# A Mamba and MoE layer on one core: the gate weights' split and one delta times u given to GpSimd, with a new written order

## The chip, the cores and the metric

The kernel runs on one core of a Trainium2 chip. The metric is the device time of one execution in microseconds (us); the median of three runs is taken. A profile is one such execution, recorded by the hardware.

The engines have short names in the profile: PE is TensorE (matmuls; PEld its weight loads), DVE is VectorE, ACT is ScalarE, POOL is GpSimd, SP is SyncE, which issues all the DMAs here. Each engine runs its own queue in order and waits for the others by semaphores.

## The reference

The input is 32 sequences of 256 tokens with 128 channels. Everything is float32.

```python
x = L0_attn_x                                  # (32, 256, 128)
x = x + mamba(layernorm(x), ...)
x = x + moe(layernorm(x), ...)

def mamba(x, W_in, conv_w, conv_b, W_x, W_dt, b_dt, A_log, D, W_out):
    xi, res = split(x @ W_in, 2)               # 256 channels each
    u = silu(causal_conv4(xi) + conv_b)
    dbc = u @ W_x                              # delta_r (8), B (16), C (16)
    delta = softplus(dbc[..., :8] @ W_dt + b_dt)
    h_t = exp(delta_t * A) * h_(t-1) + delta_t * B_t * u_t     # 16 states per channel
    y_t = sum over states of h_t * C_t
    return ((y + u * D) * silu(res)) @ W_out

def moe(x, gate_w, w1, w2):                    # 8 experts, the best 2 of each token
    scores = x @ gate_w.T
    cw = softmax over the top 2 scores, 0 for the other experts
    return sum over e of cw[:, e] * (silu(x @ w1[e].T) @ w2[e].T)
```

## The kernel before

**Tiles.** The 32 sequences are worked through in 17 tiles: tiles 0 and 16 hold one sequence, the others two (`EDGE`, `BPT`, line 306). Channels lie on the 128 partitions in two halves, c = 0 and 1. The 16 states of one half are scanned in groups of 1024 columns: two states of two sequences, or in tiles 0 and 16 four states of one sequence. So a tile of two sequences has 16 scans, tiles 0 and 16 have 8, 256 in all.

**Pieces and the order.** The work of a tile is cut into named pieces (`@piece`). `ORDER`, a list written out ahead of time (lines 47 to 284), names tile and piece: `1:sc0` is scan 0 of tile 1. At the end (line 1190) the pieces are issued in that order. An instruction only enters the queue of its own engine, so the list fixes the order on each engine, on SP's queue too; between engines only data dependences and free buffers hold an instruction back. `need` (line 527) puts a table load on ScalarE wherever the list goes over from one activation function's table to another's; so the order also sets how many of these there are (L530).

The pieces that matter here, with their lines and engines:

- `ldx`, `ldr`: loads of x (SP); two buffers. `st1..`, `sa1`: statistics of the first layernorm and their aggregation (VectorE, L538, L544); `rs1`: its scale, with a power (GpSimd, L554 to L557); `ap1`: the normalization itself (ScalarE, L563); `tr1`, `hi1`, `nl1`, `lo1`: the transposition into a high and a low float32r part (TensorE, ScalarE).
- `cv0`, `cv1`: convolution and input projection in one (TensorE, L635); `u0`, `u1`: silu (ScalarE, L649); `wx`: u @ W_x (TensorE, L658); `sb`, `rh`, `nr`, `rl`: that result for B and C, and in two parts for delta (ScalarE, L671, L685, L695); `bcd`: B and C to DRAM (SP); `rb`, `rc`: a row of B or C read back and spread over all partitions (SP, L778).
- `zz`: the product with W_dt (TensorE, L728), which needs `kdt`, the split of W_dt (VectorE, L497); `sp0`, `sp1`: softplus, giving delta (ScalarE, L739); `gp`, `gs`: the gate res and its silu (TensorE, ScalarE, L703, L718).
- `du0`, `du1`: delta times u of one channel half (GpSimd, L793) into the SBUF tile `dus`; `dp0`, `dp1`: its copy into the PSUM tile `du`, of which there is one (ScalarE, L799). Tile 0 uses `dq0` and `dq1` in their place: VectorE writes delta times u straight into PSUM (L807).
- `in0..15`: du times a row of B into PSUM (VectorE, L818); `dk0..15`: the decays exp(delta A) (ScalarE, L760; nine buffers); `sc0..15`: the scan (VectorE, L825) into one of three state buffers h; `cm0..15`: h times a row of C, in place (GpSimd, L836); `ys0..15`: h transposed and added up over states in PSUM (TensorE, L844), which frees the state buffer.
- `yc`, `yz`, `yt`, `ye`, `op`, `x2`: gate, transposition and output projection. Then the second layernorm (`st2..` to `lo2`), the router (`gt` on TensorE; `sc`, `r0` to `r3`, `rw1`, `rw2` on VectorE) and per expert `wi`, `si`, `wo`, `as`, `aa`: first product (TensorE, L1125), silu (ScalarE, L1138), second product (TensorE, L1146), scaling (ScalarE, L1158), sum (GpSimd, L1164). In the last tiles `ad` adds on VectorE (L1169).

**Weights.** They are loaded once, in the list between the first tile's pieces. Weights used in float32r are split into a high part (a cast) and a low part (the rest): `split`, line 356, on VectorE. `kgt` (line 515) splits the gate weights of the router, 128x8; they are needed first by `0:gt`. `kw0`, `kw1` split the halves of w1, `kwr` the gate half of W_in. `kdg` (line 510) makes the diagonal with D that `ys0` of each half multiplies with u.

Of the kernel before, what the change touches and what calls it, by code (L numbers as in the profile page):

```python
# [8 lines left out]
F32 = mybir.dt.float32  # L9
# [62 lines left out]
1:st22 2:sc4 2:rc4 2:cm4 0:aa7 2:rc5 2:rb6 2:rc7 2:rb7 5:ldx 2:rc12 2:rc6 1:st21 2:in5 1:st23 2:dk13 0:wo5
3:wx 3:sb 3:rh 1:x2 2:dk12 0:wo3 2:ys2 2:sc5 1:sa2 1:rs2 2:in6 3:nr 2:ys3 0:wo1 2:dk14 0:as5 3:rl 1:ap2 0:as3
2:ys4 0:wo6 2:sc6 2:cm5 2:in7 1:tr2 1:hi2 5:st10 2:sc7 1:nl2 2:ys5 2:dp1 1:lo2 2:in8 1:gt 1:sc 2:sc8 1:wi30
2:in9 1:r3 0:aa3 0:as1 1:wi10 1:si10 1:si30 2:cm6 2:cm7 0:aa5 2:ys6 2:sc9 5:st12 2:in10 1:r0 1:wi11 1:wi70
1:si11 1:wi40 0:as6 1:wi00 1:si70 1:wi20 1:si40 1:si00 1:si20 2:ys7 2:sc10 1:wi50 1:si50 2:yc0 1:wi31 1:si31
1:wi51 1:si51 2:in11 1:r1 2:rb12 2:rb14 3:zz 4:rs1 4:ap1 3:sp0 3:sp1 2:cm8 2:rc11 2:rb15 2:ys8 1:wo1 1:wi01
2:sc11 2:in12 0:aa1 2:cm9 2:rc14 3:bcd 2:rb13 2:cm10 1:r4 3:du0 2:cm11 2:dk15 3:dk2 1:rx 1:r2 1:rw0 1:rw4
2:yz0 2:ys9 2:sc12 2:cm12 0:aa6 1:wi71 1:wi60 2:ys10 2:ys11 1:si01 1:si71 1:si60 2:in13 1:rw1 2:sc13 2:rc15
2:ldr 3:rb1 2:rc13 3:rb4 3:rc0 2:in14 3:rb0 1:rw2 2:sc14 2:in15 1:rw3 2:cm13 3:rc3 3:rb3 2:cm14 1:wi61 1:si61  # L80
1:wi41 1:si41 1:wi21 1:si21 3:dk1 1:wo0 1:wo6 1:as6 3:dk3 1:as1 1:aa1 1:aa6 2:ys12 2:sc15 2:cm15 3:dp0 3:in1
5:st11 3:dk5 2:ys13 3:sc1 3:in0 2:yt0 1:wo3 1:as3 2:ye0 1:as0 3:dk0 2:px 2:ys14 3:sc0 1:wo4 2:ys15 1:wo5 3:dk6
2:yc1 3:dk4 3:dk8 3:rb2 0:sto 3:in2 5:st13 3:rc2 3:rc1 6:ldx 1:aa3 2:yz1 2:yt1 3:cm0 1:aa0 3:cm1 2:ye1 3:sc2
2:op 3:ys0 2:st20 4:tr1 3:in3 2:st21 2:st22 3:sc3 2:st23 3:in4 2:sa2 1:as4 1:wo2 3:ys1 3:sc4 3:dk7 1:as5 1:aa5
3:cm2 2:rs2 3:dk11 3:dk10 4:hi1 4:nl1 1:wo7 3:ys2 1:as2 4:lo1 2:x2 3:dk12 2:ap2 4:cv0 3:rb5 3:in5 5:sa1 3:sc5
3:rc5 3:rb7 3:rb6 3:rc4 3:rc6 2:tr2 4:u0 3:in6 6:st10 2:hi2 3:cm3 4:gp0 2:nl2 3:ys3 4:cv1 4:gs0 2:lo2 3:dk9
3:sc6 1:aa2 1:as7 3:dk13 3:cm4 5:rs1 3:du1 3:cm5 3:in7 3:dp1 3:dk15 6:st13 3:ys4 3:sc7 3:cm6 3:rc12 3:rc7 2:gt
2:sc 3:in8 2:r0 3:rb13 3:ys5 2:wi00 4:gp1 2:si00 2:wi30 4:u1 4:wx 4:gs1 2:wi60 3:ys6 3:sc8 3:cm7 5:ap1 2:si60
2:si30 4:sb 2:r1 3:in9 2:r3 3:sc9 3:ys7 2:wi20 2:si20 4:rh 2:wi70 2:wi61 4:nr 2:si70 3:yc0 4:rl 2:si61 3:dk14
3:in10 2:r2 3:sc10 2:wi50 3:cm8 3:ys8 3:cm9 3:ys9 4:zz 2:wi21 1:aa4 2:r4 2:rx 2:rw0 3:ldr 3:rc13 3:rb12 4:bcd  # L90
3:rc11 4:rb1 3:in11 4:sp0 2:wi71 4:sp1 2:wi31 2:si21 2:si31 2:si71 2:rw4 2:rw1 3:sc11 3:in12 3:cm10 3:ys10
2:wi01 5:tr1 2:wi40 2:si01 2:si50 2:si40 2:wi10 2:si10 5:hi1 2:wi41 2:wi51 2:rw2 3:sc12 4:du0 1:aa7 3:cm11
3:cm12 2:rw3 3:yz0 3:rb14 3:rc15 3:in13 3:rb15 3:rc14 4:rb4 3:sc13 3:in14 3:cm13 4:rb0 2:wi11 2:si11 2:si51
2:si41 3:ys11 2:wo2 2:wo3 3:ys12 5:nl1 3:yt0 3:sc14 4:rc0 4:rc1 3:cm14 4:dk3 4:dk2 2:as3 2:as2 2:aa3 3:ys13
2:wo1 3:ys14 2:wo0 3:in15 4:dp0 6:st11 4:rb3 3:sc15 4:in0 6:st12 3:cm15 4:rb2 2:aa2 3:ys15 4:dk0 4:sc0 4:cm0
4:in1 5:lo1 3:px 4:dk1 3:ye0 2:wo4 2:as0 2:wo5 3:yc1 3:yz1 2:as1 4:dk5 4:dk7 4:dk9 3:yt1 4:ys0 6:sa1 4:sc1
4:in2 4:sc2 4:in3 3:ye1 3:op 3:st20 4:sc3 3:st23 3:st21 3:st22 4:in4 3:sa2 4:dk4 4:dk6 2:wo7 2:aa1 2:as5
4:dk11 4:cm1 4:ys1 4:sc4 2:aa0 6:rs1 4:du1 4:dk12 2:as7 5:cv0 4:rc4 4:rc3 1:sto 3:x2 4:dk10 7:ldx 4:rc2 4:cm2
4:ys2 4:rb5 4:rb7 4:rc5 4:rb6 4:rc7 5:cv1 5:gp1 4:in5 2:aa7 2:as4 4:dk8 5:u1 5:gp0 5:gs0 3:rs2 3:ap2 5:u0
4:cm3 4:rc11 4:ys3 2:wo6 4:cm4 4:rc6 4:sc5 4:cm5 2:aa5 4:in7 3:tr2 3:hi2 5:wx 5:sb 5:rh 4:ys4 7:st10 4:sc7  # L100
3:nl2 3:lo2 4:in6 4:sc6 4:cm6 4:cm7 4:ys5 5:nr 5:rl 3:gt 3:sc 4:dp1 4:in8 5:gs1 3:wi70 3:si70 2:as6 3:wi50
3:si50 3:r3 4:sc8 3:wi00 3:si00 3:wi30 3:wi40 4:ys6 3:wi60 6:ap1 3:si30 3:r0 3:si40 4:in9 3:si60 2:aa4 4:cm8
3:r4 4:rb13 4:ldr 4:rb12 5:bcd 4:rc12 3:r1 4:sc9 4:in10 5:rb1 3:r2 4:dk13 4:ys7 4:yc0 3:rx 4:dk14 4:sc10
3:wi51 3:wi41 3:wi20 3:si41 3:si51 3:si20 4:in11 4:ys8 7:st13 4:sc11 4:in12 3:wi31 4:cm9 4:rc13 4:rb14 4:ys9
3:wi10 3:si10 3:si31 3:wi01 3:wi11 3:si11 3:wi21 3:si21 3:si01 4:cm10 2:aa6 4:yz0 3:rw0 3:rw4 4:cm11 4:sc12
4:in13 3:rw1 3:wi71 3:si71 3:wi61 3:si61 4:yt0 4:ys10 5:zz 4:sc13 4:in14 3:rw2 3:wo1 4:ye0 6:tr1 5:sp0 3:wo3
4:ys11 5:sp1 3:wo2 4:cm12 4:ys12 5:du0 4:cm13 3:rw3 4:dk15 5:dk0 5:dk1 6:hi1 6:nl1 5:dk3 3:as1 4:sc14 4:rb15
4:in15 7:st11 4:rc14 4:cm14 5:rb4 4:rc15 5:rb0 5:rb3 5:dp0 6:lo1 5:dk7 4:ys13 3:aa1 3:wo5 4:ys14 3:wo0 5:dk4
3:as5 3:as2 4:sc15 4:cm15 3:aa5 4:ys15 3:wo4 4:yc1 3:as0 4:yz1 5:dk2 5:in1 5:rc0 5:rb2 7:st12 5:sc1 5:in0
# [178 lines left out]
def mamba_moe_kernel(  # L288
# [67 lines left out]
    def split(parts, src):  # L356
        nc.vector.tensor_copy(parts[0], src)
        nc.vector.tensor_tensor(parts[1], src, parts[0].bitcast(F32), ALU.subtract)
# [913 lines left out]
```

## Time and profile before

| what | us |
|---|---|
| median of 3 runs | 1044.05 |
| lowest and highest run | 1043.04, 1046.95 |
| the profiled execution, its own time | 1043.46 |
| its span, first to last instruction | 1041.7 |
| first scan starts | 25.92 |
| last scan starts | 1002.96 |

| engine | busy us | share of the span |
|---|---|---|
| VectorE | 967.1 | 93% |
| TensorE | 952.9 | 91% |
| ScalarE | 944.7 | 91% |
| GpSimd | 901.8 | 87% |

Of VectorE's time 584.3 us are the 256 scans (2282 ns each) and 314.9 us their 256 products with B (1230 ns each). Of GpSimd's, 604.2 us are the products with C (2379 ns each).

Rows of the timeline read: start in us, duration in us, engine, source line, operation, output tile <- input tiles, shapes, count; in brackets the idle time of the engine just before, and what it waited for. Where several instructions of one kind follow each other, they are merged into one row. Rows of the waits read: who waited, for whom, us in all, how many times, the longest.

### The profile page before, as it was taken

The numbers are of one execution on the slowest core, as the hardware profiler recorded it, in microseconds if no ns is written. First come the engines' busy times: TensorE is split into PE (matmuls) and PEld (weight loads), VectorE is DVE, ScalarE is ACT, GpSimd is POOL, SyncE is SP. The second block draws the span as 40 slices with busy tenths as digits, with TensorE's granted clock in tenths as the row PEclk, the third lists the DMA queues.
The fourth block names the chain that finished last, engine by engine and source line by source line (L and its number), as shares of the span: only waits on it lengthen the run. The fifth ranks groups of instructions, "written<-read, shape, count | busy, mean of one in ns | idle before, by whom it ended". The sixth has DMA issues, their size and how long they took to land.

```text
span 1041.7 us, 18833 instructions
## 1 busy us (share of the span) xinstructions
PE 952.9 (91%) x6693; PEld 833.6 (80%) x6693; DVE 967.1 (93%) x946; ACT 944.7 (91%) x1893; POOL 901.8 (87%) x676
## 2 busy tenths in 40 slices
PE   6578789899999999999999999999989999899998
PEld 5467678879798888879888887888878788787888
DVE  4999999999999999999999999999999999999963
ACT  6889989989899999989999898989979999899975
POOL 2668888999899999998899999998989999899962
PEclk9789999999999999999999999999999999999999
DMA  7474848668476776847586685858668585865500
GB/s 234 155 258 161 284 167 274 219 215 284 172 256 189 254 257 205 282 157 260 197 266 240 209 268 174 273 175 277 222 196 272 179 279 178 269 232 197 182 11 16
DMA packets 86094, 223.75 MB, mean 215 GB/s; under 512 B 8048, under 2 KB 35312, under 8 KB 85872
## 3 DMA queue, kind: packets, MB, share of 16 engines
q1 hardware_dynamic: 86000, 222.55, 64.5%
q8 instruction: 52, 0.85, 0.3%
q14 instruction: 42, 0.34, 0.1%
HBM read 217.28 MB, written 5.24 MB: 214 GB/s over the span
## 4 chain that ended last, share of the span: by engine, by line
PE 31%; ACT 26%; DVE 21%; POOL 15%; issue 6%; DMA 1%; SPq 0%; DVEq 0%; POOLq 0%; ACTq 0%
DVE h L825 13%; ACT da L760 9%; PE pf L1125 9%; POOL h L836 9%; PE pe L1146 7%; DVE db L818 6%; PE y L844 6%; ACT L530 5%; POOL x L1164 3%; ACT so L1158 3%; PE pc L635 3%; ACT hs L1138 2%; PE po L966 1%; PE pd L658 1%; ACT xn_c L563 1%
## 5 line engine op out<-in xcount | busy, mean ns | idle before, releaser
L836 POOL TENSOR_TENSOR h<-h,rc 128x1024 f32<-128x1024 f32 x255 | 604.2, 2379 | 67.4 <-DVE h L825 56.3
L825 DVE TENSOR_TENSOR_SCAN h<-da,db 128x1024 f32<-128x1024 f32 x256 | 584.3, 2282 | 21.9 <-PE y L844 7.6
L760 ACT ACTIVATE da<-de,a_sb 128x510 f32<-128x510 f32 (+1 forms) x544 | 341.1, 718 | 0.9 <-DVE h L825 0.5
L818 DVE TENSOR_TENSOR db<-du,rb 128x1024 f32<-128x1024 f32 x256 | 314.9, 1230 | 11.2 <-ACT du L799 2.1
L844 PE MATMUL y<-ident,h 128*128 128x128 f32 x2048 | 268.8, 278 | 20.0 <-POOL h L836 19.5
L844 PEld LDWEIGHTS y<-ident,h 128*128 128x128 f32 x2048 | 237.2, 144 | 39.2 <-POOL h L836 26.7
L1146 PE MATMUL pe<-w_sb,hs 128*128 128x128 f32 x2048 | 249.1, 276 | 3.8 <-ACT so L1158 2.8
L1146 PEld LDWEIGHTS pe<-w_sb,hs 128*128 128x128 f32 x2048 | 238.8, 192 | 11.3 <-ACT so L1158 4.4
L1125 PE MATMUL pf<-xt,w_r 128*128 128x512 f32 (+1 forms) x816 | 215.8, 399 | 12.5 <-ACT hs L1138 7.3
L1138 ACT ACTIVATE hs<-pf 128x512 f32<-128x512 f32 (+1 forms) x272 | 144.6, 577 | 40.3 <-PE pf L1125 36.6
L1125 PEld LDWEIGHTS pf<-xt,w_r 128*128 128x128 f32 x816 | 138.6, 189 | 52.9 <-ACT hs L1138 19.7
L1164 POOL TENSOR_TENSOR x<-x,so 128x512 f32<-128x512 f32 (+1 forms) x126 | 157.5, 1250 | 10.5 <-ACT so L1158 9.2
L1158 ACT ACTIVATE so<-pe,cw 128x128 f32<-128x128 f32 x488 | 140.4, 393 | 6.4 <-PE pe L1146 4.1
L530 ACT ACT_TABLE_LOAD x105 | 134.7, 1283 | 1.9
L635 PE MATMUL pc<-xt_r,wc_r 128*128 128x512 f32 (+1 forms) x408 | 99.9, 396 | 1.1 <-ACT xt_r L624 1.1
L635 PEld LDWEIGHTS pc<-xt_r,wc_r 128*128 128x128 f32 x408 | 73.8, 197 | 15.4 <-issue 0.8
L862 PE MATMUL y<-dg_sb,u 128*128 128x128 f32 x256 | 36.4, 285 | 11.7 <-ACT yt L917 6.9
L862 PEld LDWEIGHTS y<-dg_sb,u 128*128 128x128 f32 x256 | 32.6, 195 | 17.0 <-ACT yt L917 10.6
L924 POOL TENSOR_TENSOR g<-yt,g 128x512 f32<-128x512 f32 (+1 forms) x33 | 40.7, 1233 | 5.6 <-ACT yt L917 2.9
L793 POOL TENSOR_TENSOR dus<-de,u 128x512 f32<-128x512 f32 (+1 forms) x32 | 39.8, 1247 | 0.0
L966 PE MATMUL po<-wo_sb,yt 128*128 128x128 f32 x256 | 32.8, 277 | 2.3 <-ACT yt L944 2.2
L966 PEld LDWEIGHTS po<-wo_sb,yt 128*128 128x128 f32 x256 | 30.8, 192 | 4.9 <-ACT yt L944 3.2
(101 smaller groups left out, 716.8 us busy)
## 6 DMA issues: line engine op xcount, KB each, us to landing
rc<-bc SPq DMA_DIRECT2D x205, 512.0 KB, 5.1
rb<-bc SPq DMA_DIRECT2D x187, 512.0 KB, 4.8
xa<-in_x SPq DMA_DIRECT2D x15, 256.0 KB, 4.4
xc<-in_x SPq DMA_DIRECT2D x15, 256.0 KB, 4.4
out<-x SPq DMA_DIRECT2D x15, 256.0 KB, 6.0
w1h<-in_w_t SPq DMA_DIRECT2D x2, 512.0 KB, 7.1
w_sb<-in_w_t SPq DMA_DIRECT2D x1, 1024.0 KB, 7.6
bc<-s SPq DMA_DIRECT2D x32, 32.0 KB, 3.1
```

The source lines that it names most:

```text
L530: nc.scalar.preload_act_table_set(SETS[which])
L635: nc.tensor.matmul(pcv, wc_r[a][:, j, c * P : (c + 1) * P], xt1_r[b][:, : nb[i], o + j : o + j + L], start=(k == 0), stop=(k == 3 * KC - 1),)
L760: nc.scalar.activation(da[:, m, :, 1:], de[:, :, 1:], AF.Exp, scale=a_sb[:, c, n : n + 1])
L818: nc.vector.tensor_mul(db, d["du"].unsqueeze(1).to_broadcast([P, gs[i], tok[i]]), rows["b", i, k])
L825: nc.vector.tensor_tensor_scan(flat(h), da_of(i, k), flat(d["db"]), 0.0, ALU.mult, ALU.add,)
L836: nc.gpsimd.tensor_tensor(h, h, rows["c", i, k], ALU.mult)
L844: nc.tensor.matmul(y[:, q, :], src[:, q * P : (q + 1) * P], ident, is_transpose=True, start=False, stop=last, skip_group_check=True,)
L1125: nc.tensor.matmul(pf, w1_r[a][:, e, f * P : (f + 1) * P], d["xt"][b], start=(k == 0), stop=(k == 2),)
L1138: nc.scalar.activation(d["hs", e][:, f, :], d["pf", e, f], AF.Silu)
L1146: nc.tensor.matmul(pe[:, q, :], hs[:, f, q * P : (q + 1) * P], w2_sb[:, e, f, :], start=(f == 0), stop=(f == FC - 1),)
L1158: nc.scalar.activation(so[:, q, :], d["pe", e][:, q, :], AF.Copy, scale=d["cw"][:, q, e : e + 1])
L1164: nc.gpsimd.tensor_tensor(x2, x2, st[i]["so", e], ALU.add)
```

## The change

`kgt` runs on GpSimd, and so does the product delta times u of channel half 1 in tile 0: `0:dq1` is replaced by `0:du1` and `0:dp1`. `dq0` stays. The tile `dus`, made so far by `du0`, is made by whichever of the two comes first. `ORDER` is replaced as a whole: but for those three pieces it names the same ones, in a different sequence from its first line to its last.

```diff
-    def split(parts, src):
-        nc.vector.tensor_copy(parts[0], src)
-        nc.vector.tensor_tensor(parts[1], src, parts[0].bitcast(F32), ALU.subtract)
+    def split(parts, src, eng=nc.vector):
+        eng.tensor_copy(parts[0], src)
+        eng.tensor_tensor(parts[1], src, parts[0].bitcast(F32), ALU.subtract)
...
     @piece("kgt")
     def _(i):
-        split([gt_r[:, k, :] for k in range(2)], stage["gt"])
+        split([gt_r[:, k, :] for k in range(2)], stage["gt"], nc.gpsimd)
...
     @piece("du1", 1)
     def _(i, c):
         d = st[i]
-        if c == 0:
+        if "dus" not in d:
             d["dus"] = pw.tile([P, DC, tok[i]], F32, tag="du", name=f"dus_{i}", bufs=1)
         nc.gpsimd.tensor_tensor(d["dus"][:, c, :], d["de"][:, c, :], d["u", c], ALU.mult)
```

The first lines of the list before:

```text
0:pm 0:ldx 0:lw0 0:lw1 0:lc0 0:lc1 1:ldx 0:ldp 0:st10 0:st11 0:sa1 0:rs1 0:ap1 0:km1 0:tr1 0:kh1 0:hi1 0:nl1
0:km0 0:kh0 0:lo1 0:kl1 1:st10 1:st11 1:st13 1:st12 0:kl0 0:kwr 0:cv1 0:cv0 1:sa1 1:rs1 3:ldx 3:st10 0:ldd
0:ldk 0:ka 0:u1 1:ap1 1:tr1 0:u0 0:wx 0:gp0 0:sb 0:rh 0:kdt 1:hi1 0:nr 0:rl 0:gs0 1:nl1 0:zz 0:pb0 1:lo1 0:sp0
0:pc0 0:l11 0:ldg 0:ld2 0:l10 2:ldx 2:st10 3:st13 0:kw0 0:kw1 2:st12 0:dq0 2:st11 2:st13 0:in0 2:sa1 0:bcd
0:rc0 0:rc3 0:rb1 0:rc1 0:rb2 0:dk0 0:dk2 0:dk1 0:sc0 0:cm0 0:in1 0:sc1 0:in2 0:kgt 0:sc2 0:dk5 0:dk3 2:rs1
2:ap1 0:kdg 0:cm1 1:gp1 1:cv1 1:cv0 1:u0 0:ys0 1:u1 0:dk4 0:ys1 1:wx 1:rh 1:sb 0:dk6 0:dk7 0:rb3 0:in3 0:dq1
0:sc3 0:in4 0:sc4 0:in6 0:rc7 0:rc2 0:cm2 0:cm3 0:ys2 1:nr 1:rl 0:sc6 1:bcd 0:ldr 0:ys3 1:zz 1:sp0 0:yc0 1:sp1
...
```

and after:

```text
0:pm 0:ldx 0:lw0 0:lc0 0:lc1 0:ldk 1:ldx 0:l11 0:ldo 0:st10 0:st11 0:sa1 0:rs1 0:km0 0:ap1 0:km1 0:tr1 1:st10
0:kh1 0:lw1 1:st12 0:ldp 0:hi1 0:kl1 0:kh0 0:nl1 0:ldd 1:st13 0:lo1 1:st11 0:kl0 0:cv1 1:sa1 1:rs1 0:ka 0:kw1
0:kwr 1:ap1 0:cv0 0:kdg 3:ldx 0:l10 2:ldx 2:st10 2:st11 0:kdt 0:u1 1:tr1 0:u0 0:wx 0:gp0 0:rh 0:sb 2:st13
1:hi1 2:st12 3:st10 0:bcd 0:nr 0:rl 1:nl1 0:gs0 0:zz 1:lo1 0:pb0 0:kw0 2:sa1 2:rs1 0:sp0 0:rc1 1:cv0 0:pc0
0:rb1 0:rc0 0:dq0 0:rb2 0:in0 0:rb3 0:rc3 0:rc2 0:dk0 1:cv1 0:ld2 0:dk6 0:sc0 0:dk1 0:in1 0:cm0 0:dk3 3:st13
0:sc1 0:dk2 0:pt 0:ys0 0:in2 0:cm1 1:gp1 0:sc2 1:u0 1:u1 0:du1 1:wx 0:in3 3:st12 0:cm2 0:ys1 0:dk4 1:gp0 0:sc3
0:dp1 0:dk5 0:ys2 0:in4 0:cm3 1:sb 2:ap1 1:bcd 0:sc4 1:rh 0:ldr 0:dk7 1:nr 0:ys3 1:rb1 0:in6 1:rb5 0:rc7 0:cm4
1:rc0 0:yc0 1:rl 1:zz 0:sc6 1:sp0 0:ys4 1:sp1 0:ldg 0:in5 0:cm6 3:st11 1:rb4 0:sc5 1:dk1 1:dk0 0:yz0 1:du0
0:in7 0:cm5 3:sa1 1:rb0 0:sc7 1:rc2 0:ys5 1:dk3 1:gs0 1:dp0 1:gs1 1:in1 0:cm7 1:dk2 1:rb6 1:sc1 1:dk4 0:kgt
1:du1 0:px 0:ys6 0:yt0 4:ldx 0:ys7 1:dk8 1:in0 0:yc1 1:rb2 0:ye0 1:sc0 0:yz1 1:rc1 0:yt1 2:tr1 0:ye1 0:op
...
```

Of the end of both lists one fact is used below: from `15:nl2` on they hold the same pieces of TensorE, in a slightly different sequence.

## The prediction

> **What bounds the kernel now.** I read the page's head first, then the timeline of VectorE (DVE) from the start, then the waits of VectorE in the middle, then those of TensorE (PE) at the end, and last ScalarE (ACT) before the first scan. The page:
>
> ```profile
> span 1041.7 us, 18833 instructions
> PE 952.9 (91%) x6693; PEld 833.6 (80%) x6693; DVE 967.1 (93%) x946; ACT 944.7 (91%) x1893; POOL 901.8 (87%) x676
> DVE  4999999999999999999999999999999999999963
> ```
>
> All engines are near full, but VectorE leads, and its empty slices lie only at the two ends. So the run has three parts: a start until the first scan (25.9 us), a middle that VectorE paces, and an end.
>
> The middle. VectorE repeats a product (L818) and a scan (L825); from scan to scan it takes 3.69 us where nothing intervenes (44.01 to 47.70, 47.70 to 51.39). Its waits from 65 to 960 us (waiter, whom it waited for, us in all, times, longest):
>
> ```profile
> DVE h L825 <- PE y L844: 7.4, 13, 1.2
> DVE db L818 <- ACT du L799: 1.6, 4, 0.6
> DVE st_c L538 <- PE po L966: 1.2, 3, 0.7
> ```
>
> With the seven smaller rows of that view they come to 14.3 us in 895: VectorE almost never stops. Whatever lengthens or shortens its queue near the start therefore shifts everything behind it.
>
> The end. From 985 us TensorE waits once, for one cast:
>
> ```profile
> PE pt_c L591 <- ACT xt L1007: 0.7, 1, 0.7
> ```
>
> That is piece 15:nl2 at 990.51. From there TensorE runs without a gap to 1038.3 us, and VectorE only adds up what it delivers.
>
> **The two operations that go.** Here are VectorE's rows (start, us taken) around them, and the GpSimd (POOL) rows of the same time:
>
> ```profile
> 29.58 2.29 DVE L825 TENSOR_TENSOR_SCAN h<-da,db 128x1024 f32<-128x1024 f32 x1
> 31.90 1.23 DVE L818 TENSOR_TENSOR db<-du,rb 128x1024 f32<-128x1024 f32 x1
> 33.04 0.16 DVE L357 CAST gt_r<-gt 128x8 fp32r<-128x8 f32 x1
> 33.24 2.26 DVE L358 TENSOR_TENSOR gt_r<-gt,gt_r 128x8 fp32r<-128x8 f32 x1
> 35.42 2.27 DVE L825 TENSOR_TENSOR_SCAN h<-da,db 128x1024 f32<-128x1024 f32 x1
> 37.73 1.23 DVE L818 TENSOR_TENSOR db<-du,rb 128x1024 f32<-128x1024 f32 x1
> 39.00 1.42 DVE L807 TENSOR_TENSOR du<-de,u 128x256 f32<-128x256 f32 x1
> 40.33 2.27 DVE L825 TENSOR_TENSOR_SCAN h<-da,db 128x1024 f32<-128x1024 f32 x1
> ```
>
> ```profile
> 33.12 2.35 POOL L836 TENSOR_TENSOR h<-h,rc 128x1024 f32<-128x1024 f32 x1
> 37.77 2.35 POOL L836 TENSOR_TENSOR h<-h,rc 128x1024 f32<-128x1024 f32 x1 [2.30 <-DVE h L825]
> ```
>
> A subtraction of eight columns takes 2.26 us and ends at 35.50; GpSimd's product beside it ends at 35.47. A product of 256 columns takes 1.42 us and ends at 40.42, 0.3 us after GpSimd's, while the same one for channel half 0 took 0.42 us at 22.86, when GpSimd stood still. So both were held up until GpSimd finished. Between these scans nothing else was late: their decays (da) were written by 32.3 us and their products just before. Scan to scan it took 5.84 and 4.91 us in place of 3.69: the two pieces cost 2.15 + 1.22 = **3.4 us** on the engine that paces the run.
>
> [...]
>
> **What is added.** On GpSimd: a product of 128x256, 0.74 us by its row of the last tile (957.33), placed between the weighings of scans 1 and 2, where GpSimd waits 2.30 us for VectorE now; and the gate split, which no GpSimd row shows: 0.21 us each by the nearest rows (128x16), 0.73 at most (128x256), so 0.4 to 1.5 us, value 0.4, placed after the last weighing of tile 0. It waits for gt's load, which moves far back on SP's queue, and queued behind it is tile 1's second du, which VectorE needs only eight scans later. On ScalarE: the copy of the delta times u into PSUM (0.43 us, row at 971.51) and one more table load (106 instead of 105 of L530, 1.28 us). The copy must wait until product 3 has read the old contents, and product 4 waits for it; one scan (2.3 us) lies between. ScalarE's new queue, from its first decay (24.18 + the 1.0 us below): five decays of 1.62 to 33.3, a table load, two u and a load (1.28 + 1.27 + 1.28) to 37.1, a decay and the copy (1.62 + 0.43) to 39.1. VectorE comes to product 4 at 26.9 + 3 x 3.69 + 2 x 0.2 (statistics) + 2.3 = 40.7. I cost all of these at nothing; if the cover is gone, the copy can hold VectorE by its length and the decay's before it, 0.43 + 1.62 = 2 us, once.
>
> **What is moved at the start.** The first scan waited 0.84 us for the decays of ScalarE, so ScalarE's chain sets its time:
>
> ```profile
> 12.28 1.28 ACT L530 ACT_TABLE_LOAD   x1
> 13.57 0.48 ACT L649 ACTIVATE u<-pc,small_sb 128x256 f32<-128x256 f32 x1
> 14.05 1.65 ACT L563 ACTIVATE xn_a<-xa,mr_a,rs_a 128x128 f32<-128x128 f32 x4
> 15.60 0.45 ACT L649 ACTIVATE u<-pc,small_sb 128x256 f32<-128x256 f32 x1
> ```
>
> The second u ends at 16.05, and the scan follows 9.87 us later over pieces whose order does not change, but for two copies of one PSUM tile that trade places. In the new order tile 1's normalization (1.65) stands ahead of the table load and both u. Its scale came at 14.01; VectorE's aggregation no longer follows the split of the gate half of w_in (10.35 to 11.01), so it comes 0.66 sooner, 13.35. Then 13.35 + 1.65 + 1.28 + 0.48 + 0.45 = 17.2: 1.15 later. One load (w_in's second half, half of 0.93 us of issue) leaves the place before the conv weights, for which VectorE waits 3.4 us now; that gives back some. I take **+1.0 us**, bounds 0 and +2 (the scale late by another 1 us, as GpSimd's power took 1.56 there and 1.01 elsewhere).
>
> The other moves stay covered. The split of w1's first loaded half goes before the gate half's, into time in which VectorE waits 5.7 us for x; the other half's split ends about 22 us, before the delta times are there (22.3). The split of W_dt now stands behind tile 2's first statistics, so behind a load that SP can issue only once tile 1's normalization is done: 15.0 + 2.8 (as 15.72 to 18.54) + 0.5 + 1.2 = 19.5; the matmul that needs it comes at 19.24 + 1.0 = 20.2. Margin 0.7 us; a slower load would add its delay to the first scan. W_out and a w1 half go ahead on SP's queue, the rows of B and C come 1 us later, 3 us before their products.
>
> **The sum.** Profiled execution 1043.46 us (span 1041.7) + 1.0 - 3.4 = **1041.1 us**. The median of the runs stands 0.6 us higher (1044.05), which I leave as scatter: they reach from 1043.04 to 1046.95. For the middle and the end I take no change, with these bounds. End: from 15:nl2 on TensorE's remaining pieces are the same in both orders, so below that point nothing is to be gained; -0.7 at best, and reordering of the last additions costs 1 at most. Middle: not under -14.3, all its waits; above, see the third rival.
>
> **Rivals.**
> 1. The middle gets better as well. The whole list is new. Adding VectorE's pitches (1.36 a product, 2.32 a scan) along both lists between the transposed sum that frees a state buffer and the scan that takes one next, I get 2.3 us on average before and 3.2 after, and under 1.5 us for 117 of 253 scans before, 37 after. The buffers (three) are what VectorE waited for most. Against it: a place in the list is no time, each engine takes only its own pieces from it. If half of the 14.3 us goes: 1041.1 - 7.2 = 1033.9.
> 2. The saving doesn't arrive: tile 1's first product waits for ScalarE's copy of du, which the new order puts behind three decays, a table load and a gate activation. Its queue goes on from 39.1: a decay, s, the normalization, rh, a decay (1.62 + 0.46 + 1.65 + 0.46 + 1.62) to 44.9, yt, rl, a load, two softplus (0.37 + 0.35 + 1.28 + 1.2) to 48.1, a load and three decays (1.28 + 3 x 1.26) to 53.2, load, gate, copy (1.28 + 0.6 + 0.59) to 55.6; scan 7 ends at 26.9 + 7 x 3.69 + 0.9 (statistics) + 2.3 = 55.9. That is 0.3 us of margin. If ScalarE is late by the 2.4 us saved, the result is 1043.5, no change.
> 3. Slower: the new order keeps state buffers longer in the middle. VectorE waited 13 times for TensorE's sums, 0.57 us on average; with three buffers each late sum stops the next scan but two. It decides against the change from 2.4 us on (four more waits), and over the bound from 2.4 + 5.2 = 7.6 us, 13 more. Were the waits three times as many, 26 x 0.57 = 14.8: 1055.9. For it: the old list leaves VectorE only 14.3 us of waits, so a new one has more to lose than to win. Against it: the margins just told.
>
> **Numbers.** Forecast 0.50, rival 1 0.25, rival 2 0.12, rival 3 0.13. About 0.5% (5.2 us, so 1038.8 and 1049.3) is what a measurement of this kernel can tell from no change. Faster: rival 1 and the lower edge of the forecast, 0.25 + 0.05 = 0.30. Slower: rival 3, 0.13. Same: the rest, 0.57. The range reaches from rival 1's price, 1034, over rival 2 to 1048, where rival 3 is left out in its upper part.
>
> **What would show it.** The first scan between 26 and 28 us; scans 1 to 4 of tile 0 each 3.7 to 4.0 us apart; scan 4 at about 42 us (44.01 now); gt_r's rows on POOL near 0.2 us; tile 1's first product near 56 us (57.45 now), with no wait for du; VectorE's waits from 65 to 960 us between 8 and 20 us; TensorE without waits from 15:nl2 on. The prediction is wrong if the first scan slips beyond 28 us, if VectorE waits for du on tile 1, or if its waits for y change by over 5 us.

## The result, and the profile after

The changed kernel takes 1053.13 us (median of five runs, 1050.23 to 1055.65), the kernel before 1044.05 in runs on the same chip (1042.70 to 1046.95): ratio 1.0077, 95% interval 1.0060 to 1.0094. It is slower by 0.8%, 12 us above the forecast and above the range. The profiled execution took 1054.68 us, its span is 1052.9; it is one of the slower of the five, so its differences to the profile before (11.2 us of span) are about 2 us larger than those of the medians.

The page of the changed kernel, head and VectorE's slices:

```profile
span 1052.9 us, 18859 instructions
PE 964.2 (92%) x6693; PEld 843.4 (80%) x6693; DVE 964.0 (92%) x943; ACT 945.0 (90%) x1895; POOL 902.9 (86%) x679
DVE  5989998999999999999999999999999999899963
```

VectorE is busy 3.1 us less than before (967.1), so the two operations did leave it, and yet the span is 11.2 us longer. The time is in its idle stretches, and the slices put the first of them early: an 8 in the third and one in the seventh, where before had nines.

VectorE's waits from 65 to 965 us (waiter, whom it waited for, us in all, times, longest):

```profile
DVE h L825 <- PE y L844: 13.8, 17, 2.9
DVE db L818 <- ACT du L799: 4.8, 6, 1.9
DVE h L825 <- ACT da L760: 2.7, 3, 1.2
```

With the smaller rows they come to 26.4 us, where before had 14.3. The waits for y, which are waits for a state buffer, went from 7.4 to 13.8; the longest is 2.9 in place of 1.2.

The start of tile 0, VectorE and then GpSimd (start, us taken, engine, line):

```profile
33.31 2.29 DVE L825 TENSOR_TENSOR_SCAN h<-da,db 128x1024 f32<-128x1024 f32 x1
...
37.00 2.29 DVE L825 TENSOR_TENSOR_SCAN h<-da,db 128x1024 f32<-128x1024 f32 x1
39.39 1.23 DVE L818 TENSOR_TENSOR db<-du,rb 128x1024 f32<-128x1024 f32 x1
40.76 2.29 DVE L825 TENSOR_TENSOR_SCAN h<-da,db 128x1024 f32<-128x1024 f32 x1
```

```profile
34.34 0.73 POOL L793 TENSOR_TENSOR dus<-de,u 128x256 f32<-128x256 f32 x1
...
56.79 0.21 POOL L358 TENSOR_TENSOR gt_r<-gt,gt_r 128x8 fp32r<-128x8 f32 x1
```

Scans 2, 3 and 4 start at 33.31, 37.00 and 40.76: 3.65 to 3.76 us apart, where before had 5.84, 4.91 and 3.68. Scan 4 comes at 40.76 in place of 44.01. The product with du waits for nothing, and the gate split costs GpSimd 0.21 us a piece. The saving of 3.3 us is there, and it is gone again later. The starts of the scans say where (n-th scan of the run, us):

| scan | before | after | difference |
|---|---|---|---|
| 0 | 25.92 | 26.00 | +0.1 |
| 4 | 44.01 | 40.76 | -3.3 |
| 8 | 58.82 | 56.38 | -2.4 |
| 32 | 149.71 | 150.60 | +0.9 |
| 40 | 179.54 | 185.66 | +6.1 |
| 112 | 454.0 | 462.9 | +8.9 |
| 224 | 882.29 | 891.20 | +8.9 |
| 232 | 911.97 | 923.87 | +11.9 |
| 255 | 1002.96 | 1014.30 | +11.3 |

So there are two steps within eight scans each, +5.2 and +3.0, and two slow losses, 4.1 us from scan 4 to 32 and 2.7 from 40 to 112. This is what stands at the first step, TensorE's rows and then VectorE's (in brackets the idle time before, and whom it waited for):

```profile
162.35 0.39 PE L728 MATMUL pz<-rh,wdt_r 128*128 128x256 f32 x2
165.96 0.79 PE L728 MATMUL pz<-rh,wdt_r 128*128 128x256 f32 x2 [3.22 <-DVE rank L1074]
166.55 3.62 PE L844 MATMUL y<-ident,h 128*128 128x128 f32 x16
```

```profile
165.49 0.41 DVE L1074 TENSOR_REDUCE rank<-psc 128x32 f32<-128x256 f32 x1
168.55 2.29 DVE L825 TENSOR_TENSOR_SCAN h<-da,db 128x1024 f32<-128x1024 f32 x1 [2.65 <-PE y L844]
```

And at the second, TensorE and then VectorE:

```profile
902.59 0.96 PE L1125 MATMUL pf<-xt,w_r 128*128 128x512 f32 x3 [2.10 <-DVE rank L1074]
```

```profile
905.41 2.29 DVE L825 TENSOR_TENSOR_SCAN h<-da,db 128x1024 f32<-128x1024 f32 x1 [2.88 <-PE y L844]
```

What the reader is to see: TensorE stands still for VectorE, and not for data. The delta of a tile's second sequence (pz) has nothing to do with the rank of the experts. But the scores of the router, `psc`, lie in one of the four buffers of the PSUM pool `w`, and so do pz, pf and the other products. `sc`, `r0`, `r1` and `r2` work on the scores in place, so the buffer is free only when VectorE has done `r2` (L1074). In the new list `r2` of tile 1 stands behind a scan and two products that follow `r0`; TensorE comes to the buffer 3.22 us too early, and the sums of h (y) stand behind it in its queue. They free the state buffers, so VectorE then waits 2.65 us for TensorE, and 0.96 for y and 1.46 for du more before scan 40. VectorE holds up TensorE, which holds up VectorE.

The ranks themselves have not moved away from their scores: from the first reduction of the scores to the rank VectorE takes 15.0 us before and 15.2 after in tile 1, and 12.6 in both in tile 13. It is TensorE's queue that brings the next user of the buffer too early. In the kernel before TensorE waits three times for a rank, 1.11 us at most, and not at tile 13. The longest, at tile 1:

```profile
164.94 0.96 PE L1125 MATMUL pf<-xt,w_r 128*128 128x512 f32 x3 [1.11 <-DVE rank L1074]
165.74 1.91 PE L844 MATMUL y<-ident,h 128*128 128x128 f32 x16
```

The end did not change. From piece 15:nl2, at 1001.40, TensorE runs on without a wait for 48.1 us (47.8 before). Its only wait there is again the one of 0.7 us for ScalarE's cast, just before.

### The profile page after: what moved, and what is told of

It reads as the page before. It is cut to its first block, busy times and chain, and to the rows that moved or that the text cites. A ratio compares the mean times of both kernels' runs of the same rounds, so it can differ in the third digit from the quotient of the medians.

```text
span 1052.9 us, 18859 instructions
## 1 busy us (share of the span) xinstructions
PE 964.2 (92%) x6693; PEld 843.4 (80%) x6693; DVE 964.0 (92%) x943; ACT 945.0 (90%) x1895; POOL 902.9 (86%) x679
## 4 chain that ended last, share of the span: by engine, by line
PE 33%; ACT 22%; DVE 17%; POOL 13%; issue 6%; DMA 3%; DVEq 0%; POOLq 0%; ACTq 0%; SPq 0%
DVE h L825 11%; PE pf L1125 9%; POOL h L836 9%; PE pe L1146 8%; ACT da L760 7%; PE y L844 7%; DVE db L818 5%; ACT L530 4%; ACT hs L1138 3%; ACT so L1158 3%; POOL x L1164 2%; DMA rc<-bc 2%; PE pc L635 2%; PE po L966 1%; PE y L862 1%
## 5 line engine op out<-in xcount | busy, mean ns | idle before, releaser
L818 DVE TENSOR_TENSOR db<-du,rb 128x1024 f32<-128x1024 f32 x256 | 314.9, 1230 | 15.2 <-ACT du L799 6.0
L844 PE MATMUL y<-ident,h 128*128 128x128 f32 x2048 | 274.2, 280 | 19.1 <-POOL h L836 18.7
L844 PEld LDWEIGHTS y<-ident,h 128*128 128x128 f32 x2048 | 240.8, 145 | 40.9 <-POOL h L836 28.1
L1125 PE MATMUL pf<-xt,w_r 128*128 128x512 f32 (+1 forms) x816 | 219.0, 402 | 19.0 <-ACT hs L1138 13.1
```

The source lines that it names most:

```text
L818: nc.vector.tensor_mul(db, d["du"].unsqueeze(1).to_broadcast([P, gs[i], tok[i]]), rows["b", i, k])
L844: nc.tensor.matmul(y[:, q, :], src[:, q * P : (q + 1) * P], ident, is_transpose=True, start=False, stop=last, skip_group_check=True,)
L1125: nc.tensor.matmul(pf, w1_r[a][:, e, f * P : (f + 1) * P], d["xt"][b], start=(k == 0), stop=(k == 2),)
```

## The theories

**A, the PSUM buffer:** the ranks of tiles 1 and 13, too late for TensorE, make most of the loss through the buffer of the scores. **B, the operations:** GpSimd is late by what it was given. **C, the clock:** the granted clock of TensorE falls to one half in more stretches than before (the page's clock row begins `9779998999`, before `9789999999`; the mean is 0.975 in place of 0.987), and late sums follow from slow matmuls; the sums at 166.55 took 3.62 us at a granted 0.50, and 16 such matmuls took 1.91 at a granted 1.00 (165.74 in the kernel before). **D, the start:** tile 1's normalization ahead of both u. All runs below were timed against the kernel before on the same chip, so their ratios are what is compared; the table after the experiments lists them.

## The experiments

**e1_kgt_only.** The old list, the gate split on GpSimd:

```diff
-        split([gt_r[:, k, :] for k in range(2)], stage["gt"])
+        split([gt_r[:, k, :] for k in range(2)], stage["gt"], nc.gpsimd)
```

> The old order, with the split of the gate weights on GpSimd; delta times u of tile 0's second half stays on VectorE. If the loss lies in the new order and the operations carry what the trace showed: kernel before - 2.15 = about 1042 us, the scans from the third on 2.1 earlier. If the operations themselves do harm (GpSimd late in tile 0, weighings later): 1044 or more.

1044.31 us, ratio 0.9992 (0.9979 to 1.0004). Scan 4 comes at 42.48, 1.5 us ahead of before; VectorE's du product, still there, now takes 1.74 us in place of 1.42. By scan 56 the lead is gone (+0.1), so the 1042 that the trace promised did not come.

**e2_old_order_both.** The old list with both operations on GpSimd:

```diff
-0:cm1 1:gp0 1:cv1 1:cv0 1:u0 0:ys0 1:u1 0:dk4 0:ys1 1:wx 1:rh 1:sb 0:dk6 0:dk7 0:rb3 0:in3 0:dq1
+0:cm1 0:du1 1:gp0 1:cv1 1:cv0 1:u0 0:ys0 1:u1 0:dk4 0:rb3 0:in3 0:dp1 0:ys1 1:wx 1:rh 1:sb 0:dk6 0:dk7
```

> The old order with both operations on GpSimd (only 0:du1, 0:dp1 and the row of B and product 3 beside them are set in new places). If order alone costs: kernel before - 3.4 = about 1040.6 us, scan 4 of tile 0 at about 40.8. If a queue that is brought forward by 3.4 us is given back by later waits whatever the order (the saving does not reach the end): 1043 to 1045.

1043.19 us, 0.9980 (0.9966 to 0.9993). Theory B falls: the same operations on GpSimd do no harm where the old list is kept, they make the kernel slightly faster. Scan 4 came only at 42.32, since my own placing let VectorE wait 1.29 us for ScalarE's copy of du, behind two decays.

**e3_new_order_neither.** The new list, both operations back on VectorE:

```diff
-        split([gt_r[:, k, :] for k in range(2)], stage["gt"], nc.gpsimd)
+        split([gt_r[:, k, :] for k in range(2)], stage["gt"])
...
-1:u1 0:du1 1:wx
...
-0:sc3 0:dp1 0:dk5
+1:u1 1:wx
...
+0:sc3 0:dq1 0:dk5
```

> The new order with both operations back on VectorE. If order and operations add up: the changed kernel + 2 to 3.4, so 1055 to 1056.5 us. If the new order's losses come because VectorE is early (it meets its waits sooner, and they end at the same time): about the changed kernel's 1053.

1053.66 us, 1.0082 (1.0060 to 1.0104), against 1.0077 with both on GpSimd. The loss is in the list: it is there without the operations (the longest wait for y is 4.3 us here). VectorE's rows of the two operations:

```profile
40.75 0.41 DVE L807 TENSOR_TENSOR du<-de,u 128x256 f32<-128x256 f32 x1
...
60.20 0.17 DVE L358 TENSOR_TENSOR gt_r<-gt,gt_r 128x8 fp32r<-128x8 f32 x1
```

At the places that the new list gives them they are not held up: 0.41 us, and 0.32 with the cast, where the kernel before had 1.42 and 2.42. GpSimd's product beside the first one starts only at 40.92, and at 60.20 GpSimd stands still. From scan 0 to scan 4 this run takes 15.01 us, the changed kernel 14.76, the kernel before 18.09: 3.1 of the 3.3 us saved there come with the new places alone. So in the new list the change of engine is worth the 0.7 us of work at most, and these runs can't resolve it: the two ratios differ by 0.0005, give or take 3 us.

**e4_ranks_early.** The changed kernel with `r1` and `r2` of two tiles directly behind `r0` (for tile 13 in the same way):

```diff
-1:r0 1:si20 1:wi51
...
-3:sp0 1:wi41 1:r1 3:sp1 2:in12 1:wo6 1:r2 3:rb1
+1:r0 1:r1 1:r2 1:si20 1:wi51
...
+3:sp0 1:wi41 3:sp1 2:in12 1:wo6 3:rb1
```

> The changed kernel with the ranks of the experts (r1, r2) of tiles 1 and 13 directly behind r0 in the list, so that VectorE frees the PSUM tile of the scores before the next scans. Theory of the PSUM slot (TensorE stands at the next matmul that wants this slot until the rank is done, and the sums that free the state buffers stand behind it): the waits of VectorE for y near 168.6 (2.65) and 905.4 (2.88) go, 5 to 8 us less than the changed kernel, 1045 to 1048. Rival, the clock of TensorE after idle stretches alone or GpSimd's lateness: within 1.5 us of the changed kernel, the waits stay.

1047.02 us, 1.0022 (1.0006 to 1.0037): 6.1 us less than the changed kernel by the medians, 5.7 by the ratios. From scan 32 to 40 it loses 1.2 us in place of 5.2, from 224 to 232 it gains 0.2 where 3.0 were lost. VectorE's rows at the first place:

```profile
161.20 0.42 DVE L1074 TENSOR_REDUCE rank<-psc 128x32 f32<-128x256 f32 x1
...
166.58 2.29 DVE L825 TENSOR_TENSOR_SCAN h<-da,db 128x1024 f32<-128x1024 f32 x1
```

The rank is done 4.3 us sooner and the scan has no wait. Theory A holds for these two places. Part of the first wait was the clock's: the 16 sums behind it take 1.91 us here, in place of 3.62 at a granted 0.50, where TensorE has stood still only 1.28 us for the rank, at 161.68. At the second place TensorE was at full clock in the changed kernel too (granted 1.00 from 902.5 to 907 us, 8 sums in 1.04 us), and VectorE waited 2.88 us all the same. Some 2 us over the kernel before are left, and more against e2.

**g1_old_ranks_late.** The reverse, in the kernel before:

```diff
-1:rx 1:r2 1:rw0 1:rw4 2:yz0
...
-2:in13 1:rw1 2:sc13
+1:rx 2:yz0
...
+2:in13 1:r2 1:rw0 1:rw4 1:rw1 2:sc13
```

Tile 13 in the same way: `13:r2` and the three behind it come after `14:in13`.

> The kernel before, with nothing changed but the ranks (r2) of tiles 1 and 13, each one to two scans later in the list (rw0 and rw4, and rw1 in tile 13, go along). In TensorE's queue a first product of an expert then waits for the rank, and the sums of h stand behind it. Theory of the PSUM slot: TensorE waits for the rank near 165 and near 898 us, about 2.8 us each time, VectorE for y right behind it, 1.5 to 3 each; 3 to 5 us over the kernel before, 1047 to 1049. Rival (the new order as a whole costs, and a rank is worth only itself): within 1 us of the kernel before.

1054.20 us, 1.0081 (1.0067 to 1.0095), more than I expected. TensorE waited 4.79 us for the rank in tile 1. But of VectorE's waits there, 2.20 us were for cw, a step of the experts' weights that my edit had itself made late; at tile 13 TensorE's wait (2.83) was for ScalarE's silu, not for the rank. So this run does not show the buffer alone.

**k3_old_one_rank_late.** Tile 1 only, with the whole chain of the weights moved along, in the kernel before:

```diff
-1:rx 1:r2 1:rw0 1:rw4 2:yz0
...
-2:in13 1:rw1 2:sc13
...
-2:in14 3:rb0 1:rw2 2:sc14 2:in15 1:rw3 2:cm13
...
-3:dk1 1:wo0
+1:rx 2:yz0
...
+2:in13 1:r2 1:rw0 1:rw4 2:sc13
...
+2:in14 1:rw1 3:rb0 2:sc14 2:in15 1:rw2 2:cm13
...
+3:dk1 1:rw3 1:wo0
```

> The kernel before with the rank of tile 1 one scan later, and the pieces of the weights that follow it (rw0, rw4, rw1, rw2, rw3) each later by as much, so that nothing of VectorE's own queue waits for them. Theory of the PSUM slot: TensorE waits for the rank 4 to 5 us near 165 (1.11 before), VectorE for the sum behind it 2.5 to 3.5; 2.5 to 4 us over the kernel before, 1048 to 1049. If the loss of the run with both ranks late came from its own broken chain of weights (VectorE waited 2.20 for cw there): within 1 us.

1051.80 us, 1.0069 (1.0048 to 1.0089). TensorE, then VectorE:

```profile
170.78 1.65 PE L1125 MATMUL pf<-xt,w_r 128*128 128x512 f32 x3 [4.82 <-DVE rank L1074]
172.22 3.62 PE L844 MATMUL y<-ident,h 128*128 128x128 f32 x16
```

```profile
170.31 0.41 DVE L1074 TENSOR_REDUCE rank<-psc 128x32 f32<-128x256 f32 x1
174.22 2.29 DVE L825 TENSOR_TENSOR_SCAN h<-da,db 128x1024 f32<-128x1024 f32 x1 [3.50 <-PE y L844]
```

One instruction of 0.41 us, one scan and one product later in the list, costs the kernel before 7 us. Nothing that VectorE does itself waits for it; TensorE does, 4.82 us, and the sums behind it then take 3.62 us, as they did at a granted 0.50 in the changed kernel. VectorE waits 3.50, and within the next eight scans 1.22 for y and 1.73 for du: 6.4 us from scan 32 to 40. That is the picture of the changed kernel in the list of before. It is also larger than I expected (2.5 to 4): what follows the first wait costs about as much as the wait.

**g4_new_filled.** e4 with idle TensorE filled in tile 0: 5, 7 and 14 such matmuls onto y, and 4 onto po, with an operand that is zero, so that they add nothing:

```diff
+            nc.tensor.matmul(y[:, j % 2, :], ident[:HR, HR:HR+1].to_broadcast([HR, P]), ident[:HR], start=False, stop=False, skip_group_check=True)
```

> The changed kernel with the ranks of tiles 1 and 13 early, and matmuls with a zero operand added onto sums that are open anyway (they add nothing) where TensorE stands idle in tile 0: 5, 7 and 14 onto y, 4 onto po. If idle TensorE is what halves its clock there, and the half clock is what makes the sums near 64 and 75 us late: the granted clock between 40 and 70 us goes from 0.66 to 0.9 or more, VectorE's waits of 2.0 and 1.1 us near there shrink, 1 to 2.5 us less than with the ranks alone (1044.5 to 1046). If the clock is not what costs: 1047, or more where a filler delays a sum.

1049.74 us, 1.0038 (1.0025 to 1.0051), no gain. A stretch of the windows of e4 and then of this run (us, busy time and count of PE, PEld, DVE, ACT, POOL, granted clock, DMA share, GB/s):

```profile
50.00:60.00 10.00, 6.26 (x28) 5.74 (x28) 8.91 (x10) 9.96 (x15) 7.55 (x7) 0.66 0.77 246
```

```profile
50.00:60.00 10.00, 8.26 (x63) 7.24 (x62) 8.94 (x11) 9.94 (x14) 9.10 (x8) 0.95 0.77 276
```

The clock rose from 0.66 to 0.95 here and from 0.83 to 1.00 between 30 and 40 us (only to 0.71 and 0.73 in the two stretches of 10 us from 40 and 60; this profile scans 1.9 us later than e4's, so the stretches hold nearly the same work). VectorE's waits for po and y behind it stayed at 2.02 and 1.06 us (2.01 and 1.07 in e4). Theory C falls for these waits: the matmuls were slow, but something else was late. At po, in e4, that was ScalarE's copy of y, which stood behind six decays until 60.74, and GpSimd's gate behind it.

**g2_new_four_waits.** e4 with four more waits of the trace mended one by one:

```diff
-1:gs0 1:dp0 1:gs1
...
-1:cm0 0:st20 0:st21 0:sa2 4:st10 0:x2 2:hi1 1:dk5 2:nl1 0:rs2 1:ys0 1:in2 2:lo1
...
-2:st20 3:in3 4:nl1
...
-6:si70 7:sc6 7:cm7 6:gt 6:si50 6:wi51 7:ys5 6:si00 7:dp1
+1:dp0 1:gs0 1:gs1
...
+1:cm0 4:st10 2:hi1 1:dk5 2:nl1 1:ys0 1:in2 0:st20 0:st21 0:sa2 0:x2 0:rs2 2:lo1
...
+3:in3 2:st20 4:nl1
...
+6:si70 7:dp1 7:sc6 7:cm7 6:gt 6:si50 6:wi51 7:ys5 6:si00
```

> The changed kernel with the ranks of tiles 1 and 13 early, and four more single places mended in the list: the copy of du of tile 1 ahead of the silu of its gate (VectorE waited 0.89), the statistics of tile 0's second layernorm behind the next product (2.01), the first of tile 2's behind the next product (1.14), the copy of du of tile 7 ahead of two silus (1.85). If what is left of the loss is the sum of such single waits: 3 to 4.5 us less than with the ranks alone, so 1042.5 to 1044 where that one gave 1047.0. If they only pass the delay on to the next wait, or if the slower clock of TensorE is what is left: 1046 to 1047.

1049.18 us, 1.0035 (1.0023 to 1.0047): no gain that can be told from e4. Three of the four waits are gone and the fourth is halved, but in their places stand others: 1.65 us for a row of B at 63.48, 1.15 for y at 74.20, 0.97 at 458.15 for a step of a layernorm's scale on GpSimd. What one place gave back, another took.

**k2_new_start_of_old.** e4, and at the start the pieces of tile 1 behind both u again, with the split of W_dt (`kdt`) ahead of tile 2's first statistics:

```diff
-0:kwr 1:ap1 0:cv0 0:kdg 3:ldx 0:l10 2:ldx 2:st10 2:st11 0:kdt 0:u1 1:tr1 0:u0 0:wx 0:gp0 0:rh
+0:kwr 0:cv0 0:kdg 3:ldx 0:l10 2:ldx 0:kdt 2:st10 2:st11 0:u1 0:u0 1:ap1 0:wx 0:gp0 1:tr1 0:rh
```

> The changed kernel with the ranks of tiles 1 and 13 early, and at the start tile 1's normalization behind both u of tile 0, as in the old order, and the split of W_dt ahead of tile 2's first statistics. The first scan started between 26.0 and 30.2 us in seven profiles of the new start, 27.3 on average, between 25.9 and 26.6 in seven of the old. If that is the normalization in ScalarE's queue, waiting for tile 1's x: first scan at or before 26.3, 1 to 1.5 us less than with the ranks alone (1045.5 to 1046). If the scatter lies in the loads themselves: no change.

1044.72 us, 1.0002 (0.9990 to 1.0014): 2.3 us less than e4 by the medians and 2.1 by the ratios, whose intervals still overlap a little, and level with the kernel before. ScalarE in the changed kernel, then ScalarE and VectorE in this run:

```profile
12.32 1.65 ACT L563 ACTIVATE xn_a<-xa,mr_a,rs_a 128x128 f32<-128x128 f32 x4 [1.69 <-POOL mr_a L557]
...
15.29 0.84 ACT L649 ACTIVATE u<-pc,small_sb 128x256 f32<-128x256 f32 x2
```

```profile
14.65 0.47 ACT L649 ACTIVATE u<-pc,small_sb 128x256 f32<-128x256 f32 x1 [2.08 <-PE pc L635]
15.02 1.64 ACT L563 ACTIVATE xn_a<-xa,mr_a,rs_a 128x128 f32<-128x128 f32 x4
```

```profile
25.39 2.29 DVE L825 TENSOR_TENSOR_SCAN h<-da,db 128x1024 f32<-128x1024 f32 x1 [1.19 <-ACT da L760]
```

In the changed kernel both u wait for tile 1's scale, and that for tile 1's x. Where that load was slower, all of tile 0 was later: over the seven profiles with this start the first scan came at 26.0 to 30.2 us, 27.3 on average; over nine with the old start at 25.9 to 26.8, 26.3 on average. The load is not all of it: in the run that starts at 30.19 (h4) the normalization begins at 14.19, 1.9 us later than in the changed kernel, and the matmuls behind it take about twice as long, 3.61 us for the eight of `pb0` in place of 1.89 at a granted 1.00. With the old start the loss from scan 8 to 16 is 0.5 us in place of 1.9. Theory D fits the rows; how much of the 2.1 us it makes, and whether the split of W_dt has a part in it, isn't separated.

**h1, h2, h4: splices of the two lists,** both operations on GpSimd, ranks of tiles 1 and 13 early, the old list with the copy of du early (g3 below). Each takes one list up to a piece, and what is left in the sequence of the other:

```diff
+h1: old list to 3:sc15, then new
+h2: new list to 3:sc15, then old
+h4: new list to 1:sc15, then old
```

> Both operations on GpSimd; the old list (with the copy of du early) up to the last scan of tile 3, from there on the pieces left in the sequence of the new list (ranks of tile 13 early). If what is left of the loss lies in the new order's first tiles, as the starts of the scans say (by tile 3 it had lost 5.8 us against its own lead, later only 1.5 more): at most 1.5 over the old order's 1041.9, 1042 to 1043.5. If it lies all along the list: 1045 or more.

> The reverse: the new list (ranks of tile 1 early) up to the last scan of tile 3, then the sequence of the old list. If the loss lies in the first tiles: 1045 to 1047.5. If it lies behind them: 1042 to 1043.

> The new list (ranks of tile 1 early) up to the last scan of tile 1, then the sequence of the old list. If tiles 0 and 1 alone lose what the starts of the scans say (2.3 of the 2.5 us of lead that the old order keeps there): about 1044. If the loss comes in tiles 2 and 3: 1042.

h1, old list first: 1046.16, 0.9997 (0.9985 to 1.0009). h2, new list through tile 3: 1049.72, 1.0050 (1.0030 to 1.0069). h4, new list through tile 1: 1048.46, 1.0030 (1.0009 to 1.0050), and this is the run whose profile starts scanning at 30.19. The heads of the new list cost most, as the scans' starts said. But its tail isn't free, as I had expected: h1 is 3.8 us above g3 by the ratios (0.0036 x 1044), and its profile loses it by single waits from 245 us on, the longest 1.98 us for du at 455. h2 and h4 came out above both of the cases that I had set down for them; each brings one wait of its own at the seam (3.18 and 3.42 us for du), so they overstate the heads.

**g3_old_order_copy_early.** e2 with the copy of du right behind tile 1's u:

```diff
-1:u1 0:dk4 0:rb3 0:in3 0:dp1 0:ys1
+1:u1 0:rb3 0:in3 0:dp1 0:dk4 0:ys1
```

> The old order with both operations on GpSimd, and ScalarE's copy of du ahead of the two decays that it stood behind, so that product 4 of tile 0 no longer waits 1.29 us for it. If an early saving reaches the end: 1.3 us less than with the copy late, about 1041.9, the scans from the fourth on 3.4 minus the later start ahead of the kernel before. If the middle takes it back: 1043 as with the copy late.

1041.91 us, 0.9961 (0.9949 to 0.9974): faster than both kernels, and by about what the operations are worth in the trace. Scan 4 comes at 40.84, 3.2 us ahead of before. The profile doesn't show the gain to the end: it is the slowest of the five runs (1043.62), had 0.5 us of lead left at scan 56 and none at the last scan (+0.1), with 10.1 us of waits for y from 65 to 965 us. The gain stands on the times of the runs alone.

**h3_old_ranks_early.** g3 with `r1`, `r2` directly behind `r0` in all tiles, here tile 2:

```diff
-2:sc 3:in8 2:r0 3:rb13
...
-4:sb 2:r1 3:in9
...
-3:in10 2:r2 3:sc10
+2:sc 3:in8 2:r0 2:r1 2:r2 3:rb13
...
+4:sb 3:in9
...
+3:in10 3:sc10
```

> The old order with both operations on GpSimd and the copy of du early, and in every tile the ranks (r1, r2) directly behind r0. TensorE waited for a rank at 165, 219 and 335 us of the kernel before (1.11, 0.68, 0.74). If the slot of the scores costs there too: those waits go, 0.5 to 1.5 us under the 1041.9 of the same order with the ranks late. If they are covered there: no change; if the 0.8 us that VectorE spends earlier on the ranks collide with something: above.

1045.08 us, 0.9997 (0.9988 to 1.0006): it loses all of g3's gain. VectorE's rows of one tile:

```profile
209.74 0.42 DVE L1059 TENSOR_TENSOR psc<-psc,sc 128x256 f32<-128x256 f32 x1
210.20 0.43 DVE L1069 TENSOR_TENSOR psc<-psc,thr 128x256 f32<-128x256 f32 x1
210.67 0.42 DVE L1074 TENSOR_REDUCE rank<-psc 128x32 f32<-128x256 f32 x1
```

Each works on what the one before has written, and starts 0.46 us after it. Spread among scans, as in g3, the first two take 0.32 us to the next start. And where such an instruction stands between a product with B and its scan, the product takes 1.14 us to the next start; where the scan follows at once, 1.36. By the profiles from the first to the last scan, h3 waits 7.5 us less than g3 (12.9 against 20.4), but its steps without waits are 10.1 us longer, 2.6 us more in all: 4.2 at the ranks and 4.4 at the products, 20 more of which have their scan right behind them.

**k1_old_sum_early.** g3 with one sum of tile 3 earlier in TensorE's queue:

```diff
-4:gp1 2:si00 2:wi30 4:u1 4:wx 4:gs1 2:wi60 3:ys6 3:sc8
+4:gp1 3:ys6 2:si00 2:wi30 4:u1 4:wx 4:gs1 2:wi60 3:sc8
```

> The old order with both operations on GpSimd and the copy of du early, and one more piece moved: the sum 6 of tile 3 ahead of two products of experts of tile 2 and a product with W_x, behind which it stood when VectorE waited 1.83 us at 213.8. If that wait is only the place of the sum in TensorE's queue: it goes, and with it the 1.7 us lost there; 1040 to 1041. If the delay passes on, as with four mended waits in the new order: 1042.

1042.48 us, 0.9972 (0.9958 to 0.9986), which can't be told from g3. The wait at 213.8 is gone; the profile has 1.69 us for a row of B at 166.56 and 1.97 for cw at 222.91 instead.

| run | list | ratio to before |
|---|---|---|
| after | new | 1.0077 |
| e3 | new, operations on VectorE | 1.0082 |
| e4 | new, two ranks early | 1.0022 |
| g2 | the same, four waits mended | 1.0035 |
| g4 | new, two ranks early, idle TensorE filled | 1.0038 |
| k2 | new, two ranks early, old start | 1.0002 |
| h4 | new to tile 1, then old | 1.0030 |
| h2 | new to tile 3, then old | 1.0050 |
| h1 | old to tile 3, then new | 0.9997 |
| e1 | old, gate split on GpSimd | 0.9992 |
| e2 | old, both operations on GpSimd, copy late | 0.9980 |
| g3 | old, both operations on GpSimd | 0.9961 |
| k1 | the same, one sum early | 0.9972 |
| h3 | g3 with all ranks early | 0.9997 |
| g1 | old, two ranks late | 1.0081 |
| k3 | old, one rank late | 1.0069 |

## Why the prediction was wrong

- **The operations, -3.4: the size came, the reason only in part.** Scan 4 at 40.76 against the 42 that was to be expected with the later start; 3.3 us were saved by then, with the scans 3.65 to 3.76 us apart. But the prediction priced the two on VectorE by their rows in the old list and took the change of engine for what ends the hold-up. e3 shows that the new places end it as well: left on VectorE, the two take 0.73 us there, and 3.1 of the 3.3 us are saved without the move. That the term came out is luck as far as the engine goes. In the old list it is the move that saves (14.69 us from scan 0 to 4 in g3, 18.09 before), and by the medians it reaches the end (g3: 0.0039 x 1044 = 4.1, interval 2.7 to 5.3; k1: 2.9). Of the hold-up the rows show this: in the kernel before GpSimd's product had begun (37.77, 2.35 us) when VectorE's came (39.00, 1.42 us), in e3 VectorE's began first (40.75, 0.41 us, GpSimd's at 40.92). Why the later one takes longer is not shown.
- **What was added, costed at nothing: right for the most part.** The gate split took 0.2 us a piece, du's copy in tile 0 made nobody wait.
- **The start, +1.0: right on average, with bounds too narrow.** The mechanism is the one named, tile 1's normalization ahead of both u; 27.3 against 26.3 us over all profiles, though only +0.1 in the changed kernel's own. The bound of +2 rested on a scale late by 1 us; once the first scan was 4.3 us later than before (h4), with a scale 1.9 us later than in the changed kernel and slow matmuls behind it (3.61 us in place of 1.89).
- **Rival 2, du of tile 1: came in small,** 0.88 us at 55.02, through the queue it named. The margin of 0.3 us was rightly called thin; this was in the forecast as no wait.
- **The middle: the step that failed.** "For the middle and the end I take no change". It changed by +14.6 us in the profile (-3.3 at scan 4, +11.3 at the last). The middle is where the prediction set down its signs of being wrong, and two of them came: VectorE waited for du on tile 1, and its waits for y rose by 6.4 us. Two ranks that TensorE needed before VectorE had them make 8.2 us of the loss by the scans' starts, and 5.7 by the ratios of the runs (e4). Rival 1 reckoned margins in VectorE's pitches alone and found the new list looser; in fact the waits for y nearly doubled. The measure saw where a sum stands in the list, and not what stands ahead of it in TensorE's queue. The trace of before had the sign of it: `pf` waited 1.11 us for the rank at 164.94, and 2.5 us for ranks in all. I read VectorE's waits, and TensorE's only at the end.
- **Rival 3, slower by state buffers: the right side, and the right place,** waits of VectorE for y. Its cause was wrong (buffers kept longer by the list) and its price per wait too: the two that decided took 2.65 and 2.88 us, not 0.57, because TensorE stood still for a buffer of PSUM, and in the first case came back at half clock (16 sums in 3.62 us, granted 0.50). I gave it 0.13 on the ground of margins that didn't look at that buffer.
- **The end, 0: right,** +0.3.

What stays open: between k2 and g3, both with both operations and without the late ranks, some 4 us remain by the ratios (0.0041 x 1044). h1 shows that most of it lies behind tile 3, spread over waits of 0.5 to 2 us of several kinds. Mending four such waits brought nothing (g2), so no single cause was found. Why the late start costs more than its own lateness (scans 8 to 16) was seen and not explained.

## What to carry to other kernels

A buffer that one engine fills and another works on in place is a lock on the first engine's queue: here TensorE stood still 3.22 us for one rank, in k3 4.82. When an order is changed, go through every pool whose buffers are shared by unlike tiles, and ask which instruction frees each one, what stands ahead of that instruction on its engine, and what stands behind the next user on the other; waits such as "TensorE for a rank" in the profile of before, even of 1 us, mark them. And a saving on an engine that paces the run is only worth what the next wait leaves of it: moving the same two operations gave 2 to 4 us in one list and nothing that the runs resolve in the other, whose places had already freed them. So change the operations and the order in separate runs, and read the price of an operation again at its new place.

## What the runs showed of the hardware

- **TensorE's clock fell after idle time, and the runs scatter with it.** The stretches at a granted 0.50 are mostly 3.41 us long or twice that (all eight in the first 400 us of the changed kernel; one of the kernel before lasts 17.07 us). In the 3.41 us ahead of a stretch TensorE was busy 0 to 1.84 us in both kernels, but for one stretch (2.98 us, ahead of 21.51 in the changed kernel); and where idle TensorE was filled, the granted clock rose from 0.66 to 0.95 (e4, g4, 50 to 60 us). In 29 runs of the kernel before, from 1042.9 to 1048.8 us, the time falls by some 4.4 us for each 0.01 of mean granted clock (correlation -0.85, which doesn't say which of the two causes the other). At equal clock (0.984, by lines fitted to these 29 and to the five runs of the changed kernel) before stands at 1045.0 and after at 1052.1, so the mean clock isn't the difference between the two. The length of a wait alone did not decide: after one of 1.29 us in g3, ahead of 206.13, 8 sums took 1.69 us and the three products behind them 1.63, where the same run has 1.04 and 0.97 at 203.01 and 211.87; after one of 2.10 us ahead of 902.59 in the changed kernel the granted clock stayed at 1.00. What decides is not shown.
- **Dependent instructions in a row on VectorE did not overlap here:** 0.46 us from start to start for one of 0.42, against 0.32 where an independent one follows; and 1.36 against 1.14 for a product of 1.23 us, by whether the scan that reads it follows at once (h3, g3). A small instruction between a product and its scan was therefore partly free here, for 0.22 us.
